# One attention kernel, one TensorE: exchanging a quarter of the exponentials of every second step

## The chip, the cores and the metric

The kernel runs on one core of one Trainium2 chip. The metric is the time of one execution on the device, in microseconds; before the change the median of three runs is 660.52 us (660.3 to 661.54). The kernel is written with an order of instructions of its own for every engine: nothing is reordered by a scheduler, and each engine (TensorE or PE, VectorE or DVE, ScalarE or ACT, GpSimd or POOL, and SyncE or SP, which issues DMAs) works through its own queue in program order.

## The reference

Eight batches of 512 rows and 512 columns; 16 heads of 32 columns. A conditioning row is projected and added to the queries and keys (not to the values); the result is added to x.

```python
x = x + attention(x, cond_1024[:, None, :], Wq, bq, Wk, bk, Wv, bv)

Q = _split_heads(x @ Wq.T + bq)
K = _split_heads(x @ Wk.T + bk)
V = _split_heads(x @ Wv.T + bv)
tQ = _split_heads(tokens @ Wq.T + bq)
tK = _split_heads(tokens @ Wk.T + bk)
cQ = Q + tQ
cK = K + tK
scores = jnp.einsum('bhqd,bhkd->bhqk', cQ, cK) / jnp.sqrt(jnp.float32(HEAD_DIM))
attn = jax.nn.softmax(scores, axis=-1)
out = jnp.einsum('bhqk,bhkd->bhqd', attn, V)
```

All of it is in float32.

## The kernel before

**Steps.** The work is cut into 32 steps, one for four heads of one batch: step t is batch t // 4, group t % 4. The main loop runs t from 1 to 28. In step t four items follow each other (`items`, i = 0 to 3). Item "V" weighs the values of step t - 1 (`weighted`); items "q", "k" and "v" make half of a projection of the next batch. A projection of two 512-column halves is done by seven block products in place of eight (a Strassen-like scheme): `four_products` in odd steps, `three_products` in even ones, and DVE and POOL add up the parts (c1, c12, c2, c22). In each item PE also makes the row scores of one query chunk of 128 rows of step t + 1 (`row_max`, lines L638 and L646), DVE takes the row maxima (L602 one head, L655 two heads), and ACT takes exponentials of those rows and sums them (`denominators`, L693). `hold` is the second half of the maxima, called later in the item.

**Two kinds of steps.** What weighs the values needs the exponentials transposed, keys on the partitions.

- In an odd step (`BLOCKED`) the row exponentials are kept in SBUF (`rows_kept`, in rooms 0 to 7 of the arena), blocks of 32 partitions are exchanged by 32 DMAs of 128 KB (`exchange`, two halves of 16; a source row of three goes by SP's queue, one by POOL's, L677), and DVE turns each 32 x 32 block in place, eight units to a step (`turn_blocks`, L666).
- In an even step the row exponentials serve for the sums alone and are written back to PSUM. The transposed scores are made afresh: `exponentials` adds the negated maxima by a small bf16 matmul (L749), multiplies keys by queries (L752), and ACT takes the exponential into the arena (L763), 512 columns for each of four heads and four key chunks. For that the maxima of all four chunks are split into three bf16 parts by POOL (`split_max`, L707 to L710) and transposed by one DMA on SP (`turn_max`, L723).

`times_v` (L774) then multiplies by the values: 16 products of 512 columns in an even step, 32 of 256 in an odd one. `send` turns the result back on DVE (L841), and POOL multiplies by the reciprocal of the sums (L842) and adds the residual (L843).

**PSUM.** All eight banks go round in a ring: `begin` gives each item its roles, `released` says in which order they come free. An even item uses roles 0 to 3 for the transposed scores, 4 to 7 for the row scores, and 0 and 3 again for the products of that item, once ACT has read them. The next even item puts its row scores into roles 6, 7, 0 and 3, so that it waits until DVE has added up the products.

**Queues around the change.** SP, in an odd step: stores, loads of x, the transpose of the maxima, loads of the residual; in an even step: first half exchange after item 0, second half after item 2. POOL, in an odd step: sums of the projections, the split; in an even step: its share of the exchanges. The x of the next batches is turned by DVE (`turn_x`, L376) and combined by POOL (`combine_x`, L393 to L397).

Block turns before the change, as units per (step less its blocked step, item):

```python
TURNED = {(-1, 3): 1, (0, 1): 2, (0, 2): 2, (0, 3): 3}
```

## Time and profile before

| | |
|---|---|
| median of 3 runs | 660.52 us |
| the profiled execution | 660.98 us |
| its span in the profile | 658.9 us |
| granted TensorE clock | 1.00 |
| a pair of an even and an odd step | 39.05 us, 14 pairs in the loop |
| start of the main loop's last even step | 591.56 us |
| data moved by DMA | 90.91 MB, mean 138 GB/s |
| packets of SP's queue / of POOL's, share of 16 DMA engines | 49.0% / 8.8% |

The profile is of one execution. A row of the timeline gives start, length, engine, line, operation, output from input, shape and count; in square brackets stands how long the engine was idle before it, and what ended that. Two records belong to each float32 matmul. Four matmuls of 32 rows or 32 columns run side by side, so the time of a group is read from the start of one group to the start of the next. A row of groups gives busy time and mean length, then idle time before. A row of DMA issues gives the median time from issue to landing.

### The profile page before, as it was taken

The page shows a single profiled execution, that of the slowest core. Times are in us where ns is not written, and L with a number is a line of the kernel's source. Part 1 is how long each engine was busy: PE and PEld are TensorE (multiplying, and loading weights), DVE is VectorE, ACT ScalarE, POOL GpSimd, SP SyncE. Part 2 cuts the span into 40 slices and gives each one's busy share as a digit, 9 for nine tenths or more (in the row PEclk, how much of TensorE's full clock was granted, in tenths as well). Part 3 has the DMA queues.
Part 4 walks back from the last instruction along what each step waited for, and adds up shares of the span by engine and source line. Part 5 has one row for each costly group of instructions (what it writes and reads, how often), then busy time and mean ns, then how long its engine had stood idle before and what let it go on. Part 6 is the DMA issues. An engine that isn't in the chain of part 4 may idle for free.

```text
span 658.9 us, 23947 instructions
## 1 busy us (share of the span) xinstructions
PE 651.5 (99%) x9568; PEld 304.1 (46%) x9568; DVE 574.6 (87%) x844; ACT 542.5 (82%) x1393; POOL 336.8 (51%) x446
## 2 busy tenths in 40 slices
PE   8999999999999999999999999999999999999997
PEld 7444443544535454444445444454553544444432
DVE  4898989989798898979989898898979888897886
ACT  2579798888989888898989979788897988889664
POOL 5552543647537464466635664464753646444340
PEclk9999999999999999999999999999999999999999
DMA  9718548385675838657484875839567582940212
GB/s 205 144 44 214 118 109 210 67 220 122 153 172 121 209 74 214 149 130 194 94 214 97 191 155 131 210 71 217 118 164 166 115 205 48 223 106 4 56 33 33
DMA packets 140818, 90.91 MB, mean 138 GB/s; under 512 B 117436, under 2 KB 126308, under 8 KB 140708
## 3 DMA queue, kind: packets, MB, share of 16 engines
q1 hardware_dynamic: 133252, 73.91, 49.0%
q0 software_dynamic: 5568, 14.95, 8.8%
q8 instruction: 75, 1.23, 0.8%
q10 hardware_dynamic: 1888, 0.52, 0.4%
q14 instruction: 35, 0.29, 0.1%
HBM read 20.27 MB, written 8.39 MB: 43 GB/s over the span
## 4 chain that ended last, share of the span: by engine, by line
PE 95%; POOL 2%; DVE 1%; DMA 1%; issue 0%; ACT 0%; ACTq 0%; DVEq 0%; POOLq 0%
PE psum L469 43%; PE psum L774 17%; PE psum L646 10%; PE psum L638 9%; PE psum L752 8%; PE psum L749 3%; PE psum L410 2%; DMA early<-in_x_dram 1%; PE psum L1227 1%; PE psum L1340 0%; PE psum L811 0%; ACT psum L693 0%; POOL wc_q L364 0%; POOL wc_q L361 0%; POOL wc_k L362 0%
## 5 line engine op out<-in xcount | busy, mean ns | idle before, releaser
L602 DVE TENSOR_REDUCE nmax<-psum 128x1 f32<-128x512 f32 x326 | 204.9, 680 | 41.7 <-PE psum L646 38.2
L693 ACT ACTIVATE psum<-psum,nmax 128x512 f32<-128x512 f32 x256 | 169.2, 665 | 46.5 <-DVE nmax L602 34.3
L763 ACT ACTIVATE arena<-psum 128x512 f32<-128x512 f32 x264 | 136.3, 603 | 29.3 <-PE psum L752 21.7
L693 ACT ACTIVATE arena<-psum,nmax 128x512 f32<-128x512 f32 x224 | 152.8, 709 | 5.8 <-issue 4.4
L666 DVE STREAM_TRANSPOSE blocks<-blocks 128x1024 f32<-128x1024 f32 x112 | 132.2, 1218 | 0.2 <-issue 0.2
L655 DVE TENSOR_REDUCE nmax<-psum 128x2 f32<-128x1024 f32 x87 | 105.3, 1212 | 1.1 <-PE psum L646 1.1
L842 POOL TENSOR_TENSOR res<-res,recs 128x512 f32<-128x512 f32 x30 | 31.4, 1048 | 121.1 <-DVE res L841 121.1
L677 POOL DMA_DIRECT2D blocks<-arena x112 | 55.9, 504 | 72.3 <-ACT arena L693 63.5
L646 PE MATMUL psum<-kT,qT 32*128 32x512 f32 x576 | 87.9, 604 | 0.0
L774 PE MATMUL psum<-arena,v 128*32 128x512 f32 x576 | 68.5, 597 | 0.0
L752 PE MATMUL psum<-qT,kT 32*128 32x512 f32 x528 | 67.9, 587 | 0.0
L638 PE MATMUL psum<-kT,qT 32*64 32x512 f32 x896 | 62.4, 613 | 0.0
L646 PEld LDWEIGHTS psum<-kT,qT 32*128 32x128 f32 x576 | 37.6, 182 | 34.1 <-DVE kT L558 6.5
L693 ACT ACTIVATION_READ_ACCUMULATOR psum<-psum,nmax 128x1 f32 x256 | 52.4, 205 | 0.0
L774 PE MATMUL psum<-blocks,v 128*32 128x256 f32 x896 | 52.1, 381 | 0.0
L693 ACT ACTIVATION_READ_ACCUMULATOR arena<-psum,nmax 128x1 f32 x224 | 50.9, 227 | 0.0
L843 POOL TENSOR_TENSOR xr<-res,xr 128x512 f32<-128x512 f32 x30 | 38.4, 1281 | 2.4
L209 POOL TENSOR_TENSOR xr<-xr,wT_q 128x512 f32<-128x512 f32 x30 | 38.3, 1280 | 0.3
L774 PEld LDWEIGHTS psum<-blocks,v 128*32 128x32 f32 x896 | 26.3, 110 | 25.0 <-ACT arena L763 10.6
L841 DVE STREAM_TRANSPOSE res<-psum 128x512 f32<-128x512 f32 x28 | 20.1, 717 | 19.0 <-issue 16.0
L469 PE MATMUL psum<-wT_v,xT 128*32 128x256 f32 x512 | 34.2, 382 | 0.0
L469 PE MATMUL psum<-wc_v,xc 128*32 128x256 f32 x512 | 33.5, 379 | 0.0
(194 smaller groups left out, 1012.3 us busy)
## 6 DMA issues: line engine op xcount, KB each, us to landing
blocks<-arena SPq DMA_DIRECT2D x336, 128.0 KB, 4.1
blocks<-arena POOLq DMA_DIRECT2D x112, 128.0 KB, 4.0
xr<-in_x_dram SPq DMA_DIRECT2D x60, 128.0 KB, 2.8
x<-in_x_dram SPq DMA_DIRECT2D x56, 128.0 KB, 2.8
out_dram<-xr SPq DMA_DIRECT2D x56, 128.0 KB, 2.3
w_q<-in_L_cond_Wq_dram SPq DMA_DIRECT2D x4, 256.0 KB
w_k<-in_L_cond_Wk_dram SPq DMA_DIRECT2D x4, 256.0 KB, 8.2
w_v<-in_L_cond_Wv_dram SPq DMA_DIRECT2D x4, 256.0 KB
```

What stands on the lines that cost most here:

```text
L469: nc.tensor.matmul(pt[r], still[:, r], moving, start=(kc == kcs[0]), stop=(kc == kcs[-1]))
L602: nc.vector.tensor_reduce(nmax[t][:, qc, j : j + 1, 0], pt, AX.X, ALU.max, negate=True)
L638: nc.tensor.matmul(pt[i * n : (i + 1) * n], qkT["q", t][r, qc * P + i * n : qc * P + (i + 1) * n], qkT["k", t][r, :], start=True, stop=True,)
L646: nc.tensor.matmul(pt, qkT["q", t][r, qc * P : (qc + 1) * P], qkT["k", t][r, :], start=True, stop=True,)
L655: nc.vector.tensor_reduce(nmax[t][:, qc, pr * 2 : pr * 2 + 2, 0], pt, AX.X, ALU.max, negate=True)
L666: nc.vector.transpose(e, e)
L677: queue.dma_start(to.rearrange("p c h s -> p (c h s)"), of)
L693: nc.scalar.activation(to, of, AF.Exp, bias=nmax[t][:, qc, j, :], accum_out=sums[t][:, qc, j, :],)
L752: nc.tensor.matmul(bank[j], qkT["k", t][r, kc * P : (kc + 1) * P], qkT["q", t][r, :], start=False, stop=True,)
L763: nc.scalar.activation(e[:, i, :], bank[pr * 2 + i], AF.Exp)
L774: nc.tensor.matmul(pt[j * HD : (j + 1) * HD, at], vs[b % 2][:, kc, (g * HG + j) * HD : (g * HG + j + 1) * HD], e, start=(kc == chunks[0]), ...
L843: nc.gpsimd.tensor_tensor(xr[t], y, xr[t], ALU.add)
```

## The change

Even steps 2 to 26 (`QUARTERED`) keep the row exponentials of their last query chunk, in the way that odd steps keep all four:

- `denominators` writes the fourth chunk's exponentials of an even step into two rooms of the arena (`quarter_rows`, rooms 12 and 13). It does so in item 2 of the odd step before.
- `exchange_quarter` moves them by 16 DMAs of 64 KB (12 on SP, 4 on POOL) into the upper halves of rooms 4 to 7 (`quarter_blocks`). In that item the second half of the maxima, the split, the transpose of the maxima and the fourth chunk's exponentials are now written out ahead of it, and the products behind.
- `turn_quarter` turns them on DVE, 1024 columns after item 0 and 1024 after item 1 of the even step.
- `weigh_quarter`, in item 2 of the even step, multiplies them by the values, 16 products of 128 columns into the upper half of role 0's bank, and DVE turns that result into a place of its own.
- `exponentials` and `times_v` of these steps take 384 columns in place of 512, `send` turns 384 columns, and POOL multiplies 128 and 384 columns apart.

Other work is moved in the same edit:

- The items of even steps come in the order V, k, q, v (t % 4 = 2) or V, v, k, q (t % 4 = 0).
- In "helped" products (all three where t % 4 = 2, q alone where t % 4 = 0) DVE writes two sums in place of three, and POOL does the third, 256 columns.
- The two x turns of an even step go from item 0 to items 1 and 2, and the first block turn of a step from behind the sums of item 3 to ahead of them. Half of `combine_x` goes from item 1 to item 3 where t % 4 = 0.
- The memset of `ones` goes to the end of the loop, since its place now holds the quarter's result.

```diff
     BLOCKED = list(range(1, T - 4, 2))
+    QUARTERED = list(range(2, T - 4, 2))
+    HELPED = ('qkv', 'q')
+    QS = S - P
...
+    def quarter_rows():
+        a = arena[:, 12:14, :].rearrange("p r c -> p (r c)")
+        return a.rearrange("p (g h s) -> p g h s", g=HG, h=HG)
+
+    def quarter_blocks():
+        return arena[:, 4:8, NP * HS :].rearrange("p a (h s) -> p a h s", h=HG)
...
     def four_products(n, b, u, dens, small, at):
...
-        nc.gpsimd.tensor_tensor(c22, c22, c12, ALU.add)
+        nc.gpsimd.tensor_tensor(c12 if n in HELPED[u] else c22, c22, c12, ALU.add)
 
     def three_products(n, b, u, dens, small, at):
         dens()
         one_, two_ = banks(at[0]), banks(at[1])
+        if n in HELPED[u]:
+            product(n, b, u, 3, two_[:, :HS])
+            product(n, b, u, 4, one_[:, :HS])
+            product(n, b, u, 5, one_[:, HS:])
...
+            nc.vector.tensor_tensor(spare, split_of(two_[:, :HS]), split_of(c22), ALU.subtract)
+            small()
...
+                nc.vector.tensor_tensor(c2, halves(one_), twice(c12), ALU.add)
+            nc.gpsimd.tensor_tensor(split_of(c12), spare, split_of(c22), ALU.add)
...
+            return
...
+    def exchange_quarter(t):
+        if t not in QUARTERED:
+            return
+        for a in range(HG):
+            for g in range(HG):
+                queue = nc.gpsimd if g in BY_POOL else nc.sync
+                of = quarter_rows()[a * BL : (a + 1) * BL, g]
+                to = quarter_blocks()[g * BL : (g + 1) * BL, a]
+                queue.dma_start(
+                    to.rearrange("p h s -> p (h s)"), of.rearrange("p h s -> p (h s)")
+                )
+
+    def turn_quarter(t, units):
+        if t not in QUARTERED:
+            return
+        for n in units:
+            e = quarter_blocks()[:, n * 2 : n * 2 + 2].rearrange("p a h s -> p a (h s)")
+            nc.vector.transpose(e, e)
+
+    def weigh_quarter(t, pt):
...
+        for kc in range(NS):
+            for j in range(HG):
+                nc.tensor.matmul(
+                    pt[j * HD : (j + 1) * HD],
+                    vs[b % 2][:, kc, (g * HG + j) * HD : (g * HG + j + 1) * HD],
+                    quarter_blocks()[:, :, j, kc * BL : (kc + 1) * BL],
+                    start=(kc == 0),
+                    stop=(kc == NS - 1),
+                )
+
+        def turn():
+            y = wT["q"][:, 0, P : 2 * P]
+            nc.vector.transpose(y, pt)
+            y_of_quarter[t] = y.rearrange("p (f e) -> p f e", e=BL)
+        return turn
...
     def exponentials(t, kc, at=None):
         bank = [bank_of(i) for i in at] if at else [banks(i) for i in range(HG)]
+        to = slice(0, QS if t in QUARTERED else S)
+        bank = [b[:, to] for b in bank]
...
-    TURNED = {(-1, 3): 1, (0, 1): 2, (0, 2): 2, (0, 3): 3}
+    TURNS_OF = {
+        (0, 0, 'e'): 'e',
+        (0, 1, 'e'): 'ex',
+        (0, 2, 'e'): 'x',
+        (0, 3, 'm'): 'b',
+        (1, 1, 'e'): 'bb',
+        (1, 2, 'e'): 'bb',
+        (1, 3, 'e'): 'bbb',
...
+    QUARTER_AT = 2
...
-        items = ["V", "q", "k", "v"]
+        items = ["V", "q", "k", "v"] if blocks else ["V", "k", "q", "v"] if t % G else ["V", "v", "k", "q"]
...
+            small = nothing
+            if not blocks and i == QUARTER_AT:
+                small = weigh_quarter(t, banks(0)[:, HS : HS + P])
+            if blocks and i == 2:
+                held()
+                held = nothing
+                dens()
+                dens = lambda js=None: None
+                exchange_quarter(t + 1)
             if item in "qkv":
-                products(t, item, blocks, held, dens, nothing)
+                products(t, item, blocks, held, dens, small)
...
-            if i == 1 and r == 0:
+            if i == 3 and r == 0:
                 combine_x(b + 1, 0, nc.gpsimd)
```

In `TURNS_OF` the key is step modulo four, item, and "m" (with the second half of the maxima, ahead of the products) or "e" (behind them); "e" as a value is a quarter turn, "x" an x turn, "b" a block turn. Steps 2 and 3 modulo four have the same entries as 0 and 1.

More of the change, by code (lines that the diff above doesn't have):

```diff
@@ L517, in four_products @@
     def four_products(n, b, u, dens, small, at):
+        if n != "v":
+            for g in range(2):
+                qkT[n, b * G + u * 2 + g] = pair_of(b * G + u * 2, n)[:, g, :]
         one_, two_ = banks(at), banks(at + 1)
@@ L687, in denominators @@
                 )
+            elif t in QUARTERED and qc == NS - 1:
+                to = quarter_rows()[:, :, j, :].rearrange("p g (c e) -> p g c e", e=BL)
             else:
@@ L746, in exponentials @@
         bank = [bank_of(i) for i in at] if at else [banks(i) for i in range(HG)]
+        to = slice(0, QS if t in QUARTERED else S)
+        bank = [b[:, to] for b in bank]
         for j in range(HG):
             r = slice(j * HD, j * HD + 3)
-            nc.tensor.matmul(bank[j], onesb[r, :], maxT[t][r, :], start=True, stop=False)
+            nc.tensor.matmul(bank[j], onesb[r, :], maxT[t][r, to], start=True, stop=False)
         for j in range(HG):
@@ L1176 @@
                     store()
+                elif what == "quarter":
+                    exchange_quarter(t + 1)
                 elif what == "residual":
```

100 lines of the change are left out of this document (79 added, 21 removed).

## The prediction

> **What bounds the kernel now.** I read the page first, then the busy time by step, then the timeline of each engine over one pair of steps. The page's rows of engines and the chain of waits:
>
> ```profile
> PE 651.5 (99%) x9568; PEld 304.1 (46%) x9568; DVE 574.6 (87%) x844; ACT 542.5 (82%) x1393; POOL 336.8 (51%) x446
> PE 95%; POOL 2%; DVE 1%; DMA 1%; issue 0%; ACT 0%; ACTq 0%; DVEq 0%; POOLq 0%
> ```
>
> TensorE fills the span and the chain. A busy PE need not be an unstalled one, so next come the windows of one even step (t = 10, starting at E) and the odd step after it (starting at O); columns are length, then busy time and instructions of each engine:
>
> ```profile
> 239.83:260.29 20.46, 20.46 (x300) 10.21 (x296) 16.93 (x28) 18.82 (x48) 11.11 (x15) 1.00 0.59 140
> 260.29:278.88 18.59, 18.59 (x300) 7.87 (x298) 18.17 (x24) 15.08 (x42) 7.63 (x11) 1.00 0.71 168
> sum 39.05, PE 39.05 PEld 18.07 DVE 35.10 ACT 33.90 POOL 18.74; mean PE 7.81 PEld 3.61 DVE 7.02 ACT 6.78 POOL 3.75
> ```
>
> A pair takes 39.05 us at a granted clock of 1.00, and DVE has 3.95 us free in it, almost all in the even step. So PE work is worth its full length, as long as DVE, which works for both sides of it, keeps up.
>
> **The change part by part.** 13 even steps (2 to 26) are touched. Below, E is the start of an even step (239.83, and 278.88 in the rows that follow) and O that of an odd one (260.29).
>
> *Exponentials, 512 to 384 columns.* PE's timeline in the even step:
>
> ```profile
> 289.49 0.40 PE L749 MATMUL psum<-wT_v,onesb 3*128 3x512 bf16 x4
> 289.71 1.03 PE L752 MATMUL psum<-qT,kT 32*128 32x512 f32 x8
> 290.57 1.33 PE L646 MATMUL psum<-kT,qT 32*128 32x512 f32 x8
> 291.83 1.07 PE L469 MATMUL psum<-xT,wc_k 128*32 128x256 f32 x16
> 295.65 1.03 PE L646 MATMUL psum<-kT,qT 32*128 32x512 f32 x8
> 296.61 1.07 PE L469 MATMUL psum<-wc_v,xT 128*32 128x256 f32 x16
> ```
>
> Start to start, the maxima's rows take 0.22 us and the scores 0.86. A quarter of 1.08 is 0.27, four times in a step: 1.08 us off PE. The row scores take 1.26 us (290.57 to 291.83) in this item and 0.96 in the next: 0.30 us of stall, for banks that DVE still holds.
>
> *Weights times V, 512 to 384 columns, and 32 new records of 128 columns.* The nearest rows (two records to each f32 matmul):
>
> ```profile
> 262.28 2.76 PE L774 MATMUL psum<-arena,v 128*32 128x512 f32 x24
> 264.97 1.11 PE L638 MATMUL psum<-kT,qT 32*64 32x512 f32 x16
> 281.57 3.21 PE L774 MATMUL psum<-blocks,v 128*32 128x256 f32 x56
> 284.71 0.39 PE L749 MATMUL psum<-wT_v,onesb 3*128 3x512 bf16 x4
> 26.47 0.65 PE L881 MATMUL psum<-wT_q,early 128*32 128x64 f32 x32
> 26.94 1.05 PE L469 MATMUL psum<-xT,wT_q 128*32 128x256 f32 x16
> ```
>
> 24 records of 512 columns take 2.69 us, so 32 take 3.59, and a quarter less saves 0.88 in the odd step's first item. Records of 256 columns take 56 ns (3.14/56), of 64 columns 15 ns (0.47/32): 128 columns lie between 0.47 and 1.8 us for 32. I take half of the 256-column row and a little for the change of shape, 0.92. Sum on PE: 1.08 + 0.88 - 0.92 = 1.04 us less per pair.
>
> The Trainium skill ("TensorE: Matmul & The Clock Gate", Back-to-back issue gap) speaks against the new product: a stream of weight load and matmul pairs is set by both, 81 ns each at 128 columns, an estimate of 2.6 us for the 32 in place of 0.92, and a pair of 39.7 us. The trace disagrees so far: its 256-column records, four column tiles side by side, cost 56 ns with a weight load each, so the sum keeps the row's value.
>
> *DVE.* Its timeline in the even step, with three rows of the odd one and the one turn of an even step's last item:
>
> ```profile
> 262.42 1.25 DVE L602 TENSOR_REDUCE nmax<-psum 128x1 f32<-128x512 f32 x2
> 266.09 1.29 DVE L602 TENSOR_REDUCE nmax<-psum 128x1 f32<-128x512 f32 x2 [0.20 <-PE psum L638]
> 277.83 3.49 DVE L666 STREAM_TRANSPOSE blocks<-blocks 128x1024 f32<-128x1024 f32 x3
> 281.24 1.25 DVE L602 TENSOR_REDUCE nmax<-psum 128x1 f32<-128x512 f32 x2
> 283.55 0.24 DVE L821 RECIPROCAL recs<-psum 128x16 f32<-128x16 f32 x1
> 284.91 0.72 DVE L841 STREAM_TRANSPOSE res<-psum 128x512 f32<-128x512 f32 x1 [1.12 <-issue]
> 285.55 1.26 DVE L376 STREAM_TRANSPOSE xT<-x 128x512 f32<-128x512 f32 x2
> 286.86 2.48 DVE L602 TENSOR_REDUCE nmax<-psum 128x1 f32<-128x512 f32 x4
> 289.26 0.41 DVE L556 TENSOR_TENSOR qT<-psum,qT 128x256 f32<-128x256 f32 x1
> 289.59 0.68 DVE L557 TENSOR_TENSOR qT<-psum,qT 128x512 f32<-128x512 f32 x1
> 290.19 0.41 DVE L558 TENSOR_TENSOR qT<-psum,qT 128x256 f32<-128x256 f32 x1
> 291.62 2.48 DVE L602 TENSOR_REDUCE nmax<-psum 128x1 f32<-128x512 f32 x4 [1.03 <-PE psum L646]
> 296.70 1.29 DVE L602 TENSOR_REDUCE nmax<-psum 128x1 f32<-128x512 f32 x2 [1.33 <-PE psum L646]
> 300.30 1.23 DVE L666 STREAM_TRANSPOSE blocks<-blocks 128x1024 f32<-128x1024 f32 x1
> ```
>
> Added per pair: two turns of 1.14 (277.83 to 281.24, over three), and one 128-column turn out of PSUM, which no row shows: between the reciprocal's 0.24 and the 512-column turn's 0.64, taken at 0.3. Taken away: 0.16 (a quarter of 0.64), and the third sum of a helped product, 0.35 us (0.33 start to start, 0.41 long), four in four steps, so 0.7 a pair. DVE grows by 1.7 to about 36.8 us busy in a pair of 38.0: it fits, if it falls in the right places. POOL takes those sums; it is 18.74 us busy in a pair.
>
> Following the even step after the change, from E: PE's first item ends at 5.56 (284.71 less 278.88, less 0.27). DVE turns the result (5.8 to 6.4), then the first quarter turn (to 7.6) where the two x turns stood, then the maxima (2.40) to 10.0, the sums (0.93 helped, 1.27 not) to 10.9 or 11.3, the second quarter turn to 12.1 or 12.5, one x turn to 12.7 or 13.1. PE reaches the new product at 11.8 and must wait for that second turn: 0.3 us where the item is helped (t = 2, 6, ..., 7 steps), 0.6 where it is not (6 steps), in place of the old 0.30. That gives back 6 x 0.3 = 1.8 us in all. What it hides under: the 1.03 and 1.33 us that DVE waits in the rows above; without that cover the whole 1.7 us of DVE would be on the path. By item 3 DVE is even with PE again, its maxima end at E + 19.8 (or 20.4), and there stands the next trouble: the first block turn now comes ahead of the sums (before, 300.30, E + 21.4).
>
> *The queues.* What that block turn needs is the first half exchange. The rows around it, and what stands ahead of it:
>
> ```profile
> 246.09 9.73 SPq L677 DMA_DIRECT2D blocks<-arena  x12
> blocks<-arena SPq DMA_DIRECT2D x336, 128.0 KB, 4.1
> 273.28 0.25 POOL L707 CAST split<-nmax 128x16 bf16<-128x16 f32 x1 [0.26 <-DVE nmax L655]
> 274.25 0.27 POOL L710 TENSOR_TENSOR split<-rest,split 128x16 bf16<-128x16 f32 x1
> 274.54 1.22 SPq L723 DMA_TRANSPOSE wT_v<-split  x1
> 275.87 2.11 SPq L196 DMA_DIRECT2D xr<-in_x_dram  x4
> L842 POOL TENSOR_TENSOR res<-res,recs 128x512 f32<-128x512 f32 x30 | 31.4, 1048 | 121.1 <-DVE res L841 121.1
> L843 POOL TENSOR_TENSOR xr<-res,xr 128x512 f32<-128x512 f32 x30 | 38.4, 1281 | 2.4
> L545 POOL TENSOR_TENSOR qT<-qT 128x256 f32<-128x256 f32 x14 | 10.3, 733 | 1.1
> ```
>
> Before, SP issues the twelve from E + 6.26 and the last lands 4.1 us after its issue, near E + 19.8. After, SP's odd step holds twelve more: the split ends 0.88 earlier (O + 13.4), the transpose of the maxima takes to 14.7, twelve issues of half the size follow, then 2.15 us of residual loads. An issue costs 0.53 (2.11/4) to 0.81 us (9.73/12, waits within); I take 0.6, nearer the row that waits for nothing: 7.2 us, done at O + 24.1, which is E + 6.4, as before. But in every second odd step (t = 5, 9, ...) POOL comes late: from O + 1.4, when DVE hands it the even step's helped Q sum, it has that (0.73), four x sums, the bias, the result's last sum and Q's 512 columns (seven of 1.28), the result's product in two parts (1.05 and an estimated 0.35), Q's 256 columns (0.73) and the split (1.24), 13.0 us. The split then ends near O + 14.4 and the exchange begins 1.0 us late. DVE then waits until E + 20.8 in place of 19.8; behind it stand the sums of that item and the next maxima. DVE would have been at its maxima at O + 1.75 against O + 2.13 now (262.42), so 0.4 is free and 0.6 goes to PE, in six steps (6, 10, ..., 26): 3.6 us. In the other seven the block turn comes at E + 20.4 or the exchange in time, with 0.9 us of slack in all. POOL's four new issues wait for ScalarE behind the split and hold back only the K and V sums, which nothing reads before the next even step. The transpose stands ahead of all twelve and keeps its place.
>
> ScalarE, 33.90 us busy in a pair, loses a quarter of 16 exponentials and writes four rows to SBUF instead of PSUM; neither bounds.
>
> Sum: 13 x 1.04 = 13.5, less 1.8, less 3.6: 8.1 us. The profiled execution (660.98 us, span 658.9) would become 652.9; it lies 0.46 above the median shown (660.52), so the median becomes 652.4.
>
> **The rivals.**
> - *The gain comes clean.* DVE's turns end before PE asks, the exchange lands in time, and the old 0.30 goes too: 13 x 1.34 = 17.4, about 643; with the landing alone in time, 649. For it: 3.95 us of DVE idle time per pair. Against it: the timeline above leaves the second turn 0.3 late. 0.17.
> - *DVE takes it all.* If 2.2 of its 3.95 us cannot be used where the turns stand (PE's own work leaves room for 1.2), the pair stays at 36.8 + 2.2 = 39.0, and the time within 1.3 us of 660.5. Against it: 1.03 + 1.33 lie just where the new turns are put. 0.08.
> - *The exchange on SP makes it slower.* Each new issue costs 0.6 + d; the first half exchange, in-order behind it, is late by 12 d more, and DVE, in-order too, carries it to PE: 6 x (0.6 + 12 d) + 7 x (12 d - 0.9, where positive). It decides from d = 0.09 (0.69 us an issue), where the 11.7 us that are left are eaten; at 0.73 the time is 666. For it: 0.81 in the same queue's row. Against it: half the bytes, at a time when the queue is quiet. 0.22.
> - *Weight loads bind the new product* at the upper bound of 1.8 us or more: 0.9 more per pair, 664. 0.03. By the 81 ns of the Trainium skill it would be 674.
> - *The transpose of the maxima lands late*, as the exchange's packets from POOL and SP run beside it: it starts at 274.54 and PE needs it at 278.88; past that, each us costs 13. With 1.0 us of stall, 666. 0.03.
>
> **How the numbers follow.** Forecast 652.4 with 0.47; its own range is 648 to 658. Faster by over 0.2% (about what a measurement of this kernel can tell from no change; 1.3 us) is forecast and clean gain, 0.64; same 0.08; slower 0.28. The range of 645 to 668 leaves out the far ends of the clean gain and of the slower cases.
>
> **What would show it.** In the changed profile: pairs of even and odd starts near 38.0 to 38.6 us; the 384-column scores near 0.65 us, the 32 new records near 0.9; weights times V of the odd step 0.9 shorter. DVE's block turn ending a wait for blocks in every second even step, and the new product waiting 0.3 to 0.6 for DVE. It is wrong if the pairs are longer than 39.05, if the new issues on SP take over 0.69 us, or if the first maxima's matmul of an even step waits for the transpose.

## The result, and the profile after

The changed kernel takes 684.38 us (median of 6 runs, 682.01 to 687.01) against 660.49 us before (6 runs beside it): a ratio of 1.0361, 95% interval 1.0328 to 1.0393. It is slower by 24 us, outside the range of 645 to 668. Its profiled execution took 682.9 us, with a span of 681.1 us.

The rows of engines and the chain of waits, on the page of the changed kernel:

```profile
PE 661.7 (97%) x9984; PEld 324.7 (48%) x9984; DVE 595.4 (87%) x855; ACT 527.4 (77%) x1393; POOL 382.4 (56%) x539
PE 68%; DMA 11%; POOL 9%; issue 3%; DVE 3%; SPq 2%; ACT 2%; ACTq 0%; DVEq 0%; POOLq 0%
```

Before, TensorE had 95% of the chain; now DMA and POOL have 20% of it. Three windows follow: the even step t = 10, the odd step t = 11 behind it, and the odd step t = 9 ahead of it (columns as before: length, then busy time and instructions of PE, PEld, DVE, ACT and POOL, granted clock, DMA share, GB/s).

```profile
246.33:269.08 22.75, 22.67 (x328) 11.89 (x328) 17.48 (x27) 17.20 (x47) 10.46 (x16) 0.92 0.70 171
269.08:286.82 17.74, 17.74 (x302) 7.87 (x299) 17.20 (x23) 14.50 (x41) 11.28 (x17) 1.00 0.74 180
225.68:246.33 20.65, 18.77 (x300) 8.25 (x296) 19.83 (x25) 15.26 (x42) 17.18 (x23) 1.00 0.73 157
```

The undisturbed odd step (t = 11) takes 17.74 us in place of 18.59: 0.85 gained. The other odd step takes 20.65, with 1.88 us in which PE does nothing. The even step takes 22.75 in place of 20.46; part of that is a clock of 0.92, which the last section returns to. The clock is not what the change costs: the run of 682.01 us had a mean granted clock of 0.999.

Item lengths, each from the start of its first matmul to the next item's, averaged over the 13 even and 13 odd steps from t = 2 to 27; the last column sums what the steps take more than before:

| steps | items before | items after | more, us |
|---|---|---|---|
| t % 4 = 2 (7) | 5.84, 4.77, 5.08, 4.78 | 5.73, 4.76, 5.85, 4.78 | +4.6 |
| t % 4 = 0 (6) | 5.83, 4.83, 5.03, 4.81 | 5.73, 4.76, 5.77, 5.06 | +4.9 |
| t % 4 = 3 (7) | 4.68, 4.63, 4.63, 4.63 | 3.83, 5.22, 4.63, 4.77 | -0.9 |
| t % 4 = 1 (6) | 4.68, 4.63, 4.64, 4.64 | 4.16, 5.98, 4.64, 5.80 | +11.9 |

The whole loop (t = 1 to 28) is 22.1 us longer. There are two losses: the odd steps gain in item 0 and give back more than that in items 1 and 3, and the even steps lose 9.4 us though TensorE has less to do in three of their four items.

**The queue and the order on POOL.** SP's queue over the end of t = 17 and the start of t = 18, a step with t % 4 = 2 that starts at 412.72:

```profile
407.26 1.22 SPq L816 DMA_TRANSPOSE wT_v<-split  x1
408.58 8.91 SPq L730 DMA_DIRECT2D arena<-arena  x12
417.54 2.20 SPq L200 DMA_DIRECT2D xr<-in_x_dram  x4
420.50 8.74 SPq L719 DMA_DIRECT2D blocks<-arena  x10
```

The twelve new issues take 0.74 us each (8.91/12), the four residual loads stand behind them, and the first half exchange starts at 420.50, 7.8 us into the step in place of 6.25. In the other steps from t = 4 to 26 it starts 7.9 to 9.2 us into the step: the twelve take 7.9 to 9.0 us there, and it starts 2.6 to 3.6 us after the first residual load. Next the same stretch on POOL, DVE and PE, in the order in which one waits for the other (the idle time ahead of a row and what ended it are in brackets):

```profile
392.04 1.25 DVE L708 STREAM_TRANSPOSE blocks<-blocks 128x1024 f32<-128x1024 f32 x1 [1.78 <-DMA blocks<-arena]
393.21 0.39 DVE L578 TENSOR_TENSOR wT_q<-psum,qT 128x256 f32<-128x256 f32 x1
393.73 0.69 DVE L584 TENSOR_TENSOR qT<-psum,qT 128x512 f32<-128x512 f32 x1
394.51 0.72 POOL L585 TENSOR_TENSOR qT<-wT_q,qT 128x256 f32<-128x256 f32 x1 [6.04 <-DVE qT L584]
395.28 2.41 PE L680 MATMUL psum<-kT,qT 32*64 32x512 f32 x16 [0.42 <-POOL qT L585]
401.49 1.27 POOL L413 TENSOR_TENSOR xT<-xT 128x512 f32<-128x512 f32 x1
406.96 0.27 POOL L803 TENSOR_TENSOR split<-rest,split 128x16 bf16<-128x16 f32 x1
412.72 0.34 PE L844 MATMUL psum<-wT_v,onesb 3*128 3x384 bf16 x4 [2.12 <-DMA wT_v<-split]
```

The late exchange holds DVE's block turn for 1.78 us. The turn stands ahead of the sums, so the sum that POOL's helped Q sum (L585) waits for is late, and PE's next row scores wait for that one. POOL then works without a break through x sums, result and projection sums up to the split, which ends at 407.23, 16.3 us into a step in which it ended at 14.2 before (274.52 - 260.29). The transpose is issued right then, and PE waits 2.12 us for it. The list of waits gives the totals (us, times, longest; PEld and PE wait for the same landing, so they are not added):

```profile
POOL qT L585 <- DVE qT L584: 74.1, 14, 6.5
PEld L844 <- DMA wT_v<-split: 12.4, 8, 2.6
DVE blocks L708 <- DMA blocks<-arena: 7.2, 6, 2.2
```

Before, no wait for the transpose or for blocks stood in this list.

### The profile page after: what moved, and what is told of

The parts are those of the page before. It is cut to its first block, busy times and chain, and to the rows that moved or that the text cites. A ratio compares the mean times of both kernels' runs of the same rounds, so it can differ in the third digit from the quotient of the medians.

```text
span 681.1 us, 25377 instructions
## 1 busy us (share of the span) xinstructions
PE 661.7 (97%) x9984; PEld 324.7 (48%) x9984; DVE 595.4 (87%) x855; ACT 527.4 (77%) x1393; POOL 382.4 (56%) x539
## 4 chain that ended last, share of the span: by engine, by line
PE 68%; DMA 11%; POOL 9%; issue 3%; DVE 3%; SPq 2%; ACT 2%; ACTq 0%; DVEq 0%; POOLq 0%
PE psum L486 26%; PE psum L871 13%; PE psum L688 10%; PE psum L847 6%; DMA wT_v<-split 6%; PE psum L680 5%; DMA blocks<-arena 4%; PE psum L844 3%; SPq L719 2%; PE psum L755 2%; DVE nmax L697 1%; PE psum L427 1%; DMA early<-in_x_dram 1%; ACT arena L858 1%; POOL qT L564 1%
## 5 line engine op out<-in xcount | busy, mean ns | idle before, releaser
L786 ACT ACTIVATE arena<-psum,nmax 128x512 f32<-128x512 f32 x276 | 187.2, 687 | 29.7 <-DVE nmax L697 9.0
L786 ACT ACTIVATE psum<-psum,nmax 128x512 f32<-128x512 f32 x204 | 134.4, 660 | 45.7 <-DVE nmax L644 37.3
L858 ACT ACTIVATE arena<-psum 128x384 f32<-128x384 f32 (+1 forms) x264 | 114.1, 519 | 39.0 <-PE psum L847 36.9
L708 DVE STREAM_TRANSPOSE blocks<-blocks 128x1024 f32<-128x1024 f32 x112 | 132.1, 1217 | 10.3 <-DMA blocks<-arena 7.2
L688 PE MATMUL psum<-kT,qT 32*128 32x512 f32 x576 | 97.7, 621 | 0.1
L680 PE MATMUL psum<-kT,qT 32*64 32x512 f32 x896 | 72.2, 613 | 1.8 <-POOL qT L585 1.8
L871 PE MATMUL psum<-arena,v 128*32 128x384 f32 (+1 forms) x576 | 57.4, 520 | 0.0
L946 POOL TENSOR_TENSOR res<-res,recs 128x512 f32<-128x512 f32 (+1 forms) x30 | 28.7, 955 | 50.9 <-DVE res L939 50.8
L847 PE MATMUL psum<-qT,kT 32*128 32x384 f32 (+1 forms) x528 | 56.8, 503 | 0.0
L585 POOL TENSOR_TENSOR qT<-wT_q,qT 128x256 f32<-128x256 f32 x14 | 10.1, 725 | 74.1 <-DVE qT L584 74.1
L786 ACT ACTIVATION_READ_ACCUMULATOR psum<-psum,nmax 128x1 f32 x204 | 41.1, 201 | 0.0
```

The costliest lines, as they stand in the source:

```text
L680: nc.tensor.matmul(pt[i * n : (i + 1) * n], qkT["q", t][r, qc * P + i * n : qc * P + (i + 1) * n], qkT["k", t][r, :], start=True, stop=True,)
L688: nc.tensor.matmul(pt, qkT["q", t][r, qc * P : (qc + 1) * P], qkT["k", t][r, :], start=True, stop=True,)
L708: nc.vector.transpose(e, e)
L786: nc.scalar.activation(to, of, AF.Exp, bias=nmax[t][:, qc, j, :], accum_out=sums[t][:, qc, j, :],)
L847: nc.tensor.matmul(bank[j], qkT["k", t][r, kc * P : (kc + 1) * P], qkT["q", t][r, to], start=False, stop=True,)
L858: nc.scalar.activation(e[:, i, :], bank[pr * 2 + i], AF.Exp)
```

## The experiments

All times are medians beside the kernel before on the same chip (660.4 to 660.7 us). "Even" and "odd" are sums over the 13 steps of each kind, in us more than before, from each profile; the changed kernel has +9.4 and +11.0.

### What the odd steps wait for

**The exchange left out** (the 16 DMAs are not issued, so the quarter's data is not exchanged).

```diff
-                exchange_quarter(t + 1)
```

> Leaves out the 16 DMAs of the quarter exchange in every odd step (so the last 128 query columns of the even steps are weighed with stale blocks); turns, products and all else stay. Three theories for the 24 us lost. A, queue: the twelve new issues on SP push the first half exchange of the next step from E + 6.3 to E + 7.8-9.2, the block turn at E + 20 waits for it, and the transpose of the maxima lands late beside the new packets: then this kernel falls to 650-660 us, the exchange starts near E + 6, no wait of DVE for blocks is left and the transpose lands in 2.4 us. B, order on POOL: the x sums behind the helped Q sum make the split of every second odd step late by themselves: then odd steps with t % 4 = 1 keep 2 us or more of stall and the time stays above 672. C, DVE is too full: the time stays near 680, with the stalls in the even items unchanged.

663.05 us, ratio 1.0038 (1.0023 to 1.0053); even +9.9, odd -7.9. The time is 3 us above the range of theory A, whose signs came but for the landing: the first half exchange starts again 5.8 to 6.3 us into the step, DVE waits for no blocks, and the transpose lands after 2.4 to 4.4 us. So the exchange carries the loss of the odd steps, some 21 us in all, and nothing of the even steps' loss.

**No quarter at all**, with the moved work kept.

```diff
-    QUARTERED = list(range(2, T - 4, 2))
+    QUARTERED = []
```

> No step is quartered (QUARTERED empty): 512 columns everywhere, no quarter rows, exchange, turns or product; the order of items, the helped sums, the places of the x turns, x sums and block turns are those of the changed kernel. A: 659-663 us, as before the change. B: the moved x sums cost by themselves, 665 or more, with waits for the transpose of the maxima in t % 4 = 1. C: like A, or some us faster than before, since DVE has fewer sums.

672.30 us, ratio 1.0177 (1.0162 to 1.0192); even +11.6, odd 0.0. The odd steps lose nothing, so the moved work alone does not delay the split enough to matter. The time lies in the range of B, but without the waits for the transpose that B asked for. The even steps have a stall of their own here: with exponentials of 512 columns, the second block product of a helped item wants the last bank before ScalarE has read it (item 1 of t = 10):

```profile
253.12 1.07 PE L486 MATMUL psum<-xc,wT_k 128*32 128x256 f32 x16 [0.29 <-ACT arena L858]
```

This is no clean price of the moved work.

**Half of the x sums one item earlier on POOL.**

```diff
-            if i == 3 and r == 0:
+            if i == 2 and r == 0:
                 combine_x(b + 1, 0, nc.gpsimd)
```

> The changed kernel with one pair of x sums on POOL called at the end of item 2, ahead of the second half exchange and of the helped Q sum, where t % 4 = 0 (in place of item 3, behind that sum). B: the split of t % 4 = 1 comes 2.6 us earlier, the wait for the transpose there goes (7 us of 12 in these steps), 672-678 us. A: the exchange still starts at E + 8 and the block turn still waits, 679-684.

665.57 us (664.87 to 674.03), ratio 1.0077 (1.0059 to 1.0096). Item 3 of the steps with t % 4 = 1 is back at 4.66 us (+0.02 in place of +1.16). The time is under both ranges. The half exchange still starts 7.7 to 9.0 us into the step and DVE still waits 6.0 us for blocks in all, but PE's waits for the transpose fall from 8.6 us to 0.9. The profiled execution took 674.03 us, 8.5 above the median, so its step sums are not used.

**The residual loads behind the first half exchange.**

```diff
-        (1, 3): ["residual"],
+        (1, 3): [],
...
-        (0, 1): [],
+        (0, 1): ["residual"],
...
-                    if 3 < t + 1 <= T - 4:
-                        load_residual(t + 1)
+                    if 3 < t <= T - 4:
+                        load_residual(t)
```

> The changed kernel with the four residual loads on SP moved from the end of the odd step, where they stand between the quarter exchange and the first half exchange, to behind that half exchange in the even step. A: the half exchange starts 2.2 us earlier, near E + 6.3, the block turn waits no more, the stalls of item 1 of the odd steps (12 us in all) go for the most part: 668-675. B: same as the changed kernel within 3 us, 681-687.

669.38 us, ratio 1.0133 (1.0100 to 1.0167); even +9.5, odd +1.4. The half exchange starts 5.8 to 6.4 us into all steps but one, DVE's waits for blocks are gone, and with them the stall in item 1 of t % 4 = 1. Item 3 there keeps +1.68: the late transpose is a cause of its own. It is not the split alone that makes it late. The split ends at O + 14.4 to 14.7 in these steps, hardly later than before the change (14.2), and with the exchange left out it ended at O + 14.4 too, where PE waited for the transpose in two steps, 0.4 and 0.8 us. Here it waits 1.5 to 2.1 us in five of the six: the transpose lands after 5.2 and 4.7 us in steps 9 and 13, against 4.1 and 2.4 with the exchange left out. So the quarter's DMAs beside it have a part in the late landing. (The profiled execution took 672.63 us, 3.3 above the median, and has a stretch at a clock of 0.50 near 487 us.)

**Both.**

> Half of combine_x one item earlier (item 2) and the residual loads behind the first half exchange, together. Theory A+B (the odd-step loss is two waits: the block turn for the exchange that is queued behind the residual loads, and the transpose that starts late behind the x sums on POOL): each part took 15 to 19 us off alone, but both cannot take off more than the odd steps lost (11.0 us over t = 2 to 27, more than was gained there by the shorter weights times V). Expected: odd steps 5 to 9 us under the kernel before, even steps still 9 to 10 us over it, 658 to 664 us. Rival K (the transpose is slow because DMA packets run beside it, whenever it is issued): odd item 3 keeps 4 us or more over the kernel before, 666 us or more.

662.59 us, ratio 1.0036 (1.0023 to 1.0049); even +10.2, odd -9.3, near what theory A+B expected. Item 0 of an odd step is 0.85 shorter, and items 1 to 3 are as before but for +0.23 in one. Each of the two edits had taken off 15 to 19 us alone; together they take off 21.8. So the late exchange and the late split feed each other, and breaking either ends most of it. The split of t % 4 = 1 now ends at O + 13.3, and in steps 9 and 13 the transpose lands after 3.0 us, beside the same DMAs as in the run ahead.

**All 16 DMAs of the quarter on SP**, with the residual loads later.

```diff
-                queue = nc.gpsimd if g in BY_POOL else nc.sync
+                queue = nc.sync
...
```

> Residual loads later, and all 16 DMAs of the quarter on SP, none on POOL: SP issues four more behind the transpose, POOL's four that stand between the split and its next sums are gone. Theory P (POOL's four DMAs, issued when the transpose is, lengthen its landing): landing of the transpose back to about 3 us, odd item 3 about 1 us shorter where t % 4 = 1, 660 to 665 us. Rival S (SP's own twelve, issued behind it, do it, or all packets alike): landing 4 to 5 us as with the residual later alone, 668 to 673 us.

682.38 us, ratio 1.0321 (1.0291 to 1.0352). Neither number was met. Four more issues of 0.72 us take 2.9 us, more than the 2.2 us that the residual loads had given up, and the half exchange starts 7.5 to 10.3 us into the step again. This is the price of the queue shown the other way round: 13 us come back with four issues. (The profiled execution took 690.48 us, 8.1 above the median, with three stretches of over 6 us at a clock of 0.50; its step sums are not used.) The transpose lands after 3.5, 3.6 and 2.4 us in steps 1, 9 and 13, against 4.2, 5.2 and 4.7 with the residual later alone; but without any exchange it took 4.1 in step 9, so what POOL's four DMAs do to it is not settled.

### Where the even steps lose

With both waits mended the kernel still lost 10.2 us in its even steps. All that follows has both edits in it.

**Scores of 512 columns kept**, of which ScalarE takes 384.

```diff
-        to = slice(0, QS if t in QUARTERED else S)
-        bank = [b[:, to] for b in bank]
+        to = slice(0, S)
+        part = slice(0, QS if t in QUARTERED else S)
...
-                nc.scalar.activation(e[:, i, :], bank[pr * 2 + i], AF.Exp)
+                nc.scalar.activation(e[:, i, :], bank[pr * 2 + i][:, part], AF.Exp)
```

> Both fixes, but the transposed scores and their maxima are still made 512 columns wide; ScalarE takes 384 of them, as in the changed kernel. TensorE has 1.08 us more work in each of 13 even steps, 14.0 us. Theory D (a saving ahead of the row scores returns as a wait for banks): 3 to 7 us more than both fixes. Rival (TensorE's own work bounds the even steps, the losses stand elsewhere): 13 to 15 us more.

667.61 us, ratio 1.0107 (1.0094 to 1.0120): 5.0 us more than both fixes, in place of 14.0 for 13 times 1.08 us of work, and in the range of theory D. The even steps, where the work lies, become only 2.8 us longer (+13.0 in place of +10.2). The timeline of PE shows why. First item 1 of t = 18 with both fixes, then the same item with the wide scores, then the item of the kernel before that starts at 284.71 (its first row stands in the prediction):

```profile
402.39 0.34 PE L844 MATMUL psum<-wT_v,onesb 3*128 3x384 bf16 x4
402.57 0.81 PE L847 MATMUL psum<-qT,kT 32*128 32x384 f32 x8
403.22 1.28 PE L688 MATMUL psum<-kT,qT 32*128 32x512 f32 x8
404.42 1.07 PE L486 MATMUL psum<-xT,wc_k 128*32 128x256 f32 x16
```

```profile
406.19 0.40 PE L844 MATMUL psum<-wT_v,onesb 3*128 3x512 bf16 x4
406.42 1.03 PE L847 MATMUL psum<-qT,kT 32*128 32x512 f32 x8
407.28 1.03 PE L688 MATMUL psum<-kT,qT 32*128 32x512 f32 x8
408.24 1.07 PE L486 MATMUL psum<-xT,wc_k 128*32 128x256 f32 x16
```

```profile
285.80 1.02 PE L646 MATMUL psum<-kT,qT 32*128 32x512 f32 x8
286.76 1.07 PE L469 MATMUL psum<-xT,wc_q 128*32 128x256 f32 x16
```

From the item's first matmul to its first block product: 2.03, 2.05 and 2.05 us. The shorter scores are 0.27 us faster, and the row scores behind them take 1.20 us in place of 0.96. What they wait for stands on DVE, first with both fixes, then with the wide scores:

```profile
402.59 0.72 DVE L939 STREAM_TRANSPOSE res<-psum 128x512 f32<-128x512 f32 x1 [1.11 <-issue]
```

```profile
406.39 0.72 DVE L939 STREAM_TRANSPOSE res<-psum 128x512 f32<-128x512 f32 x1 [1.12 <-issue]
```

The result's turn starts 0.20 us after PE's last product in both and frees its bank 0.72 later, 0.92 after the item's start. PE is ready for that bank at 0.83 (narrow) or 1.09 (wide); less 0.96 of work, the row scores run freely from 1.07 (404.42 - 0.96 - 402.39) or 1.09. So the loop from TensorE's last product through DVE and back takes about 1.07, and the scores of 512 columns had just covered it.

**The new product ahead of the row scores**, and the second quarter turn ahead of DVE's sums in item 1.

```diff
                 exponentials(t, i)
+                if i == QUARTER_AT:
+                    small = weigh_quarter(t, banks(0)[:, QS:])
...
-        (0, 1, 'e'): 'ex',
+        (0, 1, 'm'): 'e',
+        (0, 1, 'e'): 'x',
```

> Both fixes, and the new product stands in item 2 ahead of the row scores instead of behind them (columns 384 to 512 of the bank whose first 384 are being read by ScalarE), with the second quarter turn ahead of DVE's sums in item 1. Theory D (the time that the shorter scores save on TensorE comes back as waits for banks that VectorE frees): 0.87 us of independent TensorE work between the scores and the row scores gives VectorE that time, so the item 2 excess of 0.5 to 0.8 us per even step goes, 4 to 7 us less than both fixes: 653 to 659 us. Rival F (VectorE is simply full in an even step; only its sum counts): the same time as both fixes within 2 us, with the wait standing in another item.

670.86 us, ratio 1.0153 (1.0140 to 1.0166); even +17.9, odd -7.8. Item 2 became longer, not shorter. The new wait, and the row of ScalarE that ends it:

```profile
414.59 1.08 PE L755 MATMUL psum<-arena,v 128*32 128x128 f32 x32 [0.57 <-ACT arena L858]
```

```profile
414.05 1.64 ACT L858 ACTIVATE arena<-psum 128x384 f32<-128x384 f32 x4 [0.34 <-PE psum L847]
```

The product writes columns 384 to 512 of a bank whose first 384 ScalarE is reading, and starts when the first of the four exponentials is done. The time is outside both ranges, and neither reading of the even steps was tested by it.

**The x turns in DVE's gap of 1.11 us.**

```diff
-        (0, 0, 'e'): 'e',
-        (0, 1, 'e'): 'ex',
-        (0, 2, 'e'): 'x',
+        (0, 0, 'm'): 'xx',
+        (0, 0, 'e'): 'e',
+        (0, 1, 'e'): 'e',
...
```

> Both fixes, and VectorE's two x turns of an even step stand in item 0 ahead of the result's turn, where it waits 1.11 us for TensorE, instead of behind the quarter turn in item 1 and behind the sums in item 2. VectorE has the same work, 1.26 us of it in a gap. Theory L (VectorE and TensorE wait for each other at fixed places, and it is the place of VectorE's work that counts): 0.3 to 0.8 us less per even step, 652 to 659 us. Rival (the even-step stalls hang on the second quarter turn and the last product alone, not on the x turns behind them): within 1.5 us of both fixes, 661 to 664 us.

664.55 us, ratio 1.0058 (1.0046 to 1.0071): 2.0 more than both fixes, outside both ranges and nearer to the rival's. The x turns were not what TensorE waited for.

**The new product behind item 2's first block product.**

```diff
             product(n, b, u, 3, two_[:, :HS])
+            if weigh is not None:
+                small = weigh()
+                dens()
...
```

> Both fixes, and the new product stands behind the first block product of item 2 instead of ahead of it. That block product (0.87 us) needs nothing from the second quarter turn, so the 0.46 us that TensorE waits for that turn should be covered, if the wait is for the turn: 13 times 0.4 to 0.5, 656 to 658 us. Rival: VectorE, which is later then by nothing, still frees the next banks at the same time, and the wait comes back in item 3: 661 to 664 us.

661.65 us, ratio 1.0017 (1.0008 to 1.0026). In the seven steps with t % 4 = 2, item 2 is 0.15 shorter than with both fixes and item 3 is 0.21 longer; the rival was the nearer. The wait went on to ScalarE, whose row maxima's exponentials overwrite the quarter's rooms and so stand behind the new product.

**Both of these**, then **with all products helped** (`HELPED = ('qkv', 'qkv')`).

> Both edits, the x turns in the gap and the new product behind the first block product. If the two waits are separate: the sum of what the two take off alone, 646 to 655 us. If one VectorE chain sets both: no more than the better of the two.

> The same, and all three products are helped in both kinds of even steps: VectorE has 0.35 us less in each of two items where t % 4 = 0, POOL 0.73 more in each. If VectorE still bounds those steps: 2 to 4 us less than without. If POOL's sums then come late for the split in the odd step behind: as much or more.

662.93 us, ratio 1.0041 (1.0027 to 1.0055), and 670.21 us, ratio 1.0146 (1.0132 to 1.0159). No gain adds up, and less work for DVE (0.35 us in twelve items) made it 7.3 us slower: item 3 of t % 4 = 0 is 0.48 longer than without, and item 1 of the odd step behind it 0.51.

**The short sum last.** In short_last and short_last_gap the helped products subtract their third block (c22) after DVE has overwritten it, so another sum comes out; instructions, sizes and waits are of the same kind.

```diff
-            product(n, b, u, 3, two_[:, :HS])
             product(n, b, u, 4, one_[:, :HS])
+            if weigh is not None:
+                small = weigh()
+                dens()
             product(n, b, u, 5, one_[:, HS:])
+            product(n, b, u, 3, two_[:, :HS])
...
```

> Both fixes, and in every product of an even step the sum of 256 columns (0.4 us) is VectorE's last instead of the one of 512 (0.7 us): the products come in the order 4, 5, 3 (or 5, 4, 3), the new product stands behind the first of them, its result in the bank that ScalarE frees last. Theory T (the row scores wait for the end of VectorE's last sum, which begins when TensorE's last product ends; the changed order of helped sums made that tail 0.3 us longer while the shorter exponentials took 0.27 us of its cover): some 0.25 to 0.3 us less in each item with such a tail, 3 items of 7 steps and 2 of 6, less the part that stalls now for nothing: 654 to 658 us. Rival F (VectorE's sum of work bounds the even step): 661 to 664 us.

> The same with no helped sums: VectorE does all three sums of every product, 0.35 us more in 27 items, POOL 0.73 less in each. Theory T: the tail is as short, only VectorE's greater work can cost: within 3 us of short_last, either way. Rival F: 5 to 9 us more than short_last.

> The same as short_last, with the first of the two x turns (0.63 us) in the 1.11 us that VectorE waits ahead of the result's turn, instead of behind the second quarter turn. If the row scores and maxima of item 2 wait for VectorE there: 1 to 4 us less than short_last. If not: within 1 us of it.

661.66 us, ratio 1.0013 (1.0004 to 1.0022); 663.55, ratio 1.0046 (1.0033 to 1.0058); 661.75, ratio 1.0017 (1.0008 to 1.0026). Against both fixes the shorter tail is worth 0.9 us in place of 4 to 8: item 2 of t % 4 = 2 falls from 5.85 to 5.51 us, and item 3 rises from 4.78 to 4.98. ScalarE's row in short_last shows where that went, and PE's row scores of item 3 behind it:

```profile
410.32 0.69 ACT L788 ACTIVATE arena<-psum,nmax 128x512 f32<-128x512 f32 x1 [1.22 <-PE psum L757]
```

```profile
412.79 1.50 PE L690 MATMUL psum<-kT,qT 32*128 32x512 f32 x8
414.21 1.07 PE L486 MATMUL psum<-wT_v,xc 128*32 128x256 f32 x16
```

ScalarE waits for the new product (L757 there), then takes four such exponentials, to 413.0 (0.67 us apart), while PE begins the row scores of item 3 at 412.79 and takes 1.42 us for them in place of 0.96. 0.35 us more of DVE work in each of 27 items (9.5 us) costs 1.9: DVE's sum of work is not the bound.

**The quarter turns earlier on DVE**, then also the order 5, 4, 3 in item 2 of t % 4 = 0.

```diff
-        (0, 0, 'e'): 'e',
-        (0, 1, 'e'): 'ex',
+        (0, 0, 'm'): 'e',
+        (0, 1, 'm'): 'e',
+        (0, 1, 'e'): 'x',
...
```

> Both fixes, and the two quarter turns stand earlier on VectorE: the first in the 1.11 us that it waits ahead of the result's turn of item 0, the second behind the maxima of item 1 and ahead of its sums; the x turns stand behind the sums of items 1 and 2. No work is added or taken away. Theory T (fixed places where one engine waits for another; the quarter turn's place decides): the second turn ends some 2.4 us earlier, the new product finds it done, ScalarE's last exponentials of the step start 0.4 us earlier, 0.4 to 0.5 us less in each of 13 even steps, 655 to 658 us. Rival F (VectorE is full): 661 to 664 us. If the quarter's data has not landed for the earlier turns: VectorE waits for arena there, 665 us or more.

> The same, and in item 2 of the six steps with t % 4 = 0 the block products come in the order 5, 4, 3 with the sum of 256 columns last, so that the tail behind the last product is 0.4 us in place of 1.0 (two sums wait there now, as VectorE's first sum waits until both products of the bank are done). Theory T: 0.3 to 0.6 us less in six steps, 2 to 4 us less than turn_in_gap. Rival F: the same within 1 us.

675.32 us, ratio 1.0226 (1.0212 to 1.0240), and 676.45, ratio 1.0243 (1.0229 to 1.0257). The first time lies in the range that was expected if the quarter's data had not landed, but neither turn waits for the data there; the second lies just outside both of its ranges. The turn fills the gap, and the gap opens again behind it. Rows of DVE and then of PE, in turn_in_gap:

```profile
412.51 2.48 DVE L644 TENSOR_REDUCE nmax<-psum 128x1 f32<-128x512 f32 x4 [1.15 <-PE psum L688]
414.92 1.23 DVE L744 STREAM_TRANSPOSE arena<-arena 128x1024 f32<-128x1024 f32 x1
416.07 0.38 DVE L578 TENSOR_TENSOR wT_k<-psum,kT 128x256 f32<-128x256 f32 x1
```

```profile
416.51 1.94 PE L688 MATMUL psum<-kT,qT 32*128 32x512 f32 x8 [0.31 <-DVE wT_k L578]
```

DVE now waits 1.15 us for the row scores of item 1, and the second turn then stands between their maxima and the sums for which TensorE waits in item 2. That item is 0.9 to 1.1 us longer in each of the 13 steps.

No version beat the kernel before.

## Why the prediction was wrong

Between the forecast of 652.4 and the result of 684.38 lie 32 us. In steps 2 to 27 some 19 of them stand in the odd steps (11.0 lost, where 13 x 0.88 - 3.6 = 7.8 were to be gained) and some 10 in the even ones (9.4 lost, where 13 x 0.16 - 1.8 = 0.3 were to be gained). By size the second and third failed steps below count most; the runs show them as one loop.

- **Weights times V, 0.88 less in the odd step's first item:** right. 0.85 us, on average over all odd steps, with both fixes.
- **The new product, 0.92 with bounds of 0.47 and 1.8:** right. It takes 0.87 us from its start to the next group in the rows with both fixes (409.40 to 410.27). The 81 ns a record of the Trainium skill ("TensorE: Matmul & The Clock Gate", Back-to-back issue gap) do not hold for this shape; it is 27 ns.
- **The give-back of 0.3 or 0.6 at the product:** right on average, by luck. Item 2 was to become 0.65 longer where it is helped (0.92 - 0.27) and 0.95 where it is not; it is 0.77 and 0.74 longer. In the rows with both fixes the wait ahead of the new product is 0.46 us in the helped kind, in place of 0.3, and 0.39 in the other, in place of 0.6.
- **"A quarter of 1.08 is 0.27, four times in a step: 1.08 us off PE":** the first step that failed. The matmuls are 0.27 shorter, but in items 0, 1 and 3 the time is not: with both fixes these change by -0.03 to -0.06, -0.02 to -0.07 and 0.00 to +0.24. That is about 0.8 in each even step, 10 to 11 of the forecast's 13.5 us. The wide scores show it directly: 14.0 us of work are worth 5.0. The step looked for stalls that were there before (the 0.30 of item 2) and not for how close the others were. The profile before had it, in rows of which two are quoted with the forecast: the item starts at 284.71, the result's turn ends at 284.91 + 0.72 = 285.63, and the row scores start at 285.80 (286.76 less 0.96). There were 0.17 us between, less than the 0.27 to be taken.
- **SP's issues, "I take 0.6", and "2.15 us of residual loads":** the second. The issues take 0.66 to 0.75 us, 0.70 in the mean of the 13 steps, just past the 0.69 at which the rival *The exchange on SP makes it slower* was to decide; and the half exchange starts 2.6 to 3.6 us after the first residual load, in place of 2.15. Together that makes it late also where POOL is in time: in t = 12, ahead of which the split had ended at O + 13.4 as forecast, it starts 8.9 us into the step in place of 6.4. The mechanism was that rival's; its price of 666 us was not, since it ended at the block turn. What it left out comes in the next two points.
- **"From O + 1.4, when DVE hands it the even step's helped Q sum":** the third. POOL's sum overwrites what DVE's 512-column sum (L584) reads, so it waits for that and not for the 256-column one ahead of it. In t = 17 it starts at O + 3.5 (394.51 - 390.97), because L584 stood behind the late block turn; where no block turn was late, in the run with the residual loads later, it starts at O + 1.7. The split then ended at O + 14.7 to 17.3 in the steps with t % 4 = 1, in place of the O + 14.4 forecast.
- **The rival *The transpose of the maxima lands late*, 0.03:** it happened, up to 2.12 us at a time, because the transpose was issued late and landed later (2.5 to 5.5 us, in the steps whose landing the profile has). Packets beside it, the rival's own reason, had a part, as the run with the residual loads later shows; with both fixes it landed after 3.0 us beside the same packets, so they are not the whole of it. The chance was too low by far: the forecast kept "the transpose stands ahead of all twelve and keeps its place" and did not carry POOL's lateness, which it had worked out, through to the landing.
- ***DVE takes it all***: not as stated. Adding 9.5 us of DVE work cost 1.9, and taking 4.2 off made it slower.
- **The place of the waits:** forecast for steps 6, 10, ..., 26. DVE's waits for blocks stand for the most part at the end of steps with t % 4 = 0 instead, ahead of the odd steps in which POOL is late. Behind steps with t % 4 = 2 there are two, 1.4 us after t = 22 and 0.4 after t = 26. That the late transpose had already moved these steps, and PE and DVE with them, fits the rows but was not tried.

What stays open: whether some order of the even step keeps the 10 us. Ten arrangements gave 661.65 to 676.45 us; where a trace was followed, the wait had moved to another of the three engines. That the loop through DVE takes the gain in item 1 is shown by the two timelines; for items 0 and 3 only the lengths show it.

## What to carry to other kernels

Ahead of taking work off the busiest engine, measure how long its next step's resource has been free when that step starts: where that is less than the cut, the cut comes back as a wait, without a stall in the profile of before. Price a new batch of DMAs by what is queued behind it, in-order, on the issuing engine, and follow the lateness through every engine until it meets itself again; here a late exchange made POOL late, which made the next exchange late. When two edits take off 15 and 19 us alone and 22 together, look for one loop behind both.

## What the runs showed of the hardware

- **An issue costs nearly the same for half the bytes.** In the changed kernel the median issue on SP takes 589 ns for a DMA of 64 KB and 593 for one of 128 KB, both between parts of SBUF. Longer ones lie among them: twelve of 64 KB take 8.91 us of the queue in the rows above, twelve of 128 KB took 9.73 before. The Trainium skill ("DMA: Bandwidth & Descriptors", Rules for kernel authors) says to coalesce small transfers, those under 64 KB being mostly overhead; these rows show the same of the issue, at 64 KB still.
- **The transpose's landing varies.** The same DMA of split maxima lands after 2.5 to 5.5 us in the changed kernel (2.4 to 3.6 before). The quarter's DMAs beside it have a part (5.2 and 4.7 us with them, 4.1 and 2.4 without, the split ending at the same place); the whole of what sets it was not found.
- **A busy PE hides waits.** With 13.5 us less to do by the forecast's prices, PE's busy time is 651.3 us with both fixes (651.5 before). The Trainium skill ("Perfetto Trace Analysis", its opening note) calls matmul busy time a bad metric of how close a kernel is to its roofline, because matmuls are pipelined; the trace agrees that it says little: the row scores that waited for a bank count as busy. From the page of the profile with both fixes:

```profile
PE 651.3 (99%) x9984; PEld 324.7 (49%) x9984; DVE 595.6 (90%) x855; ACT 527.1 (80%) x1393; POOL 383.6 (58%) x539
```

- **The clock fell after some stalls and not after others.** Windows of the changed kernel ahead of and behind the 1.88 us wait at the start of t = 10:

```profile
244.00:246.33 2.33, 0.45 (x11) 0.00 (x0) 2.33 (x3) 1.46 (x4) 2.25 (x4) 1.00 0.78 174
248.00:250.00 2.00, 2.00 (x26) 0.53 (x21) 0.91 (x2) 1.21 (x4) 0.97 (x1) 0.50 0.41 102
250.00:252.00 2.00, 2.00 (x46) 1.09 (x42) 1.68 (x3) 1.72 (x5) 0.00 (x0) 0.86 0.39 98
```

The granted clock is 0.50 from 248 to 250 us and 0.86 in the next two, and the item takes 7.06 us in place of 5.43 (t = 6 and 18). It fell once more in t = 13; the two cost some 3 us in all, an estimate from these windows and the like ones of t = 13. The longer wait of 2.12 us at 412.72 did not lower it, and in the run with half of the x sums earlier it fell to 0.50 between 430 and 434 us though no wait of PE in that step was over 0.42. The Trainium skill ("TensorE: Matmul & The Clock Gate", What's actually happening) puts the fall after about 3.4 us of idling; PE's wait here was 1.88 us, so the length of one wait does not tell; what else counts was not tried.
